# Two VectorE instruction forms in the routed octets of a relational graph convolution

## The chip, the cores and the metric

The kernel runs on one core of one Trainium2 chip. The metric is the device time of one execution, in microseconds, as the median of several runs. The core has five engines that run side by side: TensorE (PE; its weight loads are PEld), VectorE (DVE), ScalarE (ACT), GpSimd (POOL) and SyncE (SP). Each runs its own instructions in order; semaphores order work between engines. SBUF and PSUM are the two on-chip memories.

## The reference

The input is a graph with 12,500 nodes of 128 features and 200,000 edges in the order of their destination, each of one of 8 relations. Two layers of a relational graph convolution run one after the other, then a residual and a layer norm:

```python
def _rgcn_conv(x, src, dst, et, basis, comp, root, bias):
    W = einsum('rb,bio->rio', comp, basis)          # 8 matrices 128x128
    msgs = einsum('ni,rio->nro', x, W)[src, et]     # a row for each edge
    seg = dst * 8 + et
    mean = segment_sum(msgs, seg) / maximum(count(seg), 1)
    return mean.reshape(N, 8, 128).sum(1) + x @ root + bias
h = x
for l in range(2):
    h = relu(_rgcn_conv(h, src, dst, et, basis[l], comp[l], root[l], bias[l])) + h
return layernorm(x + h)
```

So each edge brings the row of its source node to a segment (destination, relation), weighted by one over the segment's count.

## The kernel before

The edges are cut into tiles of 128, one edge per partition, and eight tiles make an octet (`Q` is 8; there are 196 octets). A plan (`Plan`) records every operation with the cells that it reads and writes, puts in the semaphore waits, and then emits each engine's instructions in the recorded order.

In the first layer POOL gathers the source rows of a tile from the input with one indirect DMA (L752, `rows<-in_x_dram,idx`); its index column lies in SBUF. Behind each such gather `pause` (L709) waits for its previous pause and then writes zeros over 256 bytes per partition of an unused tile (L712, `blank<-`), which no engine reads. PE multiplies the rows by scaled one-hots that DVE makes (L1218), then by the relations' matrices (L1343), and places them at their nodes. As blocks of nodes become ready, a table `y_d` is written to HBM: for the second layer, the rows of every node times each of the eight matrices.

In the second layer two kinds of octets alternate. Most gather their eight tiles' rows from `y_d` (L752, `rows<-y_d,idy`), and DVE makes their one-hots by `slot_hots` (L1177, L1180) from a row of column numbers, `cols`, that lies in PSUM. Every third octet from 7 to 190, 62 in all, is routed (`ROUTED`, L510): its rows are not gathered but picked on the chip from `hT`, the first layer's result, which stays in SBUF, and POOL gathers only one tile of leftovers for it (`gather_left`, L774 to L782).

A routed octet's edges have been sorted, during the first layer, into 32 groups of three or four node blocks with 32 places each. It is worked off in four steps (`NU`), by `route_step` (L1930):

- `compare` (L1824) builds the one-hots that pick the rows. `bits`, an SBUF tile, holds for each of the step's 256 places (8 groups of 32) the edge's node within its block, as f16, the same in all partitions; `nodes` holds in column j each partition's own node number in the group's j-th block, as f32. For j = 0, 1, 2 one instruction compares the 256 places with column j and writes 256 f32 numbers to `hot_b` (home: the tile `dm`). In the last step of an octet, two groups have a fourth block: one more instruction over 64 places.
- `pick_rows` (L1865) multiplies these one-hots by `hT` on PE (L1880).
- `slots_in` (L1841) makes, for each of the step's two tiles of 128 picked rows, a one-hot of 640 columns: `segs`, the column numbers as f16 in SBUF (home: `y_row`), compared with the row's segment and scaled by the row's weight. Segment and weight are columns `v` and `NTL + v` of a small f32 SBUF tile (home: `comp_sb` or `sel`).
- `add_up` (L1891) multiplies the picked rows by these one-hots on PE (L1900) into two PSUM banks, and after the fourth step `relate` (L1918) applies the matrices.

At step t, `route_step` emits the comparison of step t+1, the picking of step t, the one-hots of step t−1 and the sums of step t−2. There are 248 steps. The line `steps_of.setdefault(FROM + t * EVERY // NU, [])` (L1951, `EVERY` 3, `NU` 4) spreads four steps over three octets, so that two of the four come together in one octet. POOL's gathers run up to five octets ahead (`AHEAD`, seven buffers `rows`).

Of the kernel before, what the change touches and what calls it, by code (L numbers as in the profile page):

```python
# [13 lines left out]
ALU = mybir.AluOpType  # L14
# [415 lines left out]
def ordered_path(  # L430
# [25 lines left out]
    nc = tc.nc  # L456
    P = 128
# [36 lines left out]
    CAP = 32  # L494
# [5 lines left out]
    NTL = NGR // BU  # L500
# [3 lines left out]
    SEG = R * NW  # L504
# [85 lines left out]
    def part_of(n, *cell):  # L590
        nonlocal free_at
        free_at += n
        assert free_at <= at
        sort_c.append(cell)
        return arena[:, free_at - n:free_at], cell
# [21 lines left out]
    left_b, idl_b, wl_b, nodes_b = (part_of(n, c) for n, c in ((4 * NR, "left"), (NR, "idl"), (NR, "wl"), (4, "nodes")))  # L617
# [57 lines left out]
    def vec(emit, reads=(), writes=()):  # L675
        plan.add("DVE", emit, reads, writes)
# [20 lines left out]
    def in_turn(emits):  # L697
        def emit():
            for e in emits:
                last = e()  # L700
            return last

        return emit
# [774 lines left out]
    nodes = nodes_b[0][:, :4]  # L1478
# [262 lines left out]
    segs = segs_b[0].bitcast(F16)  # L1741
# [6 lines left out]
    def new(cell):  # L1748

        if cell in touched:  # L1750
            return [cell]
        touched.add(cell)
        return [cell] + old[cell]
# [66 lines left out]
    def tiles_at(u):  # L1820

        return range(u * TU, (u + 1) * TU)

    def compare(t):  # L1824

        i, u = t // NU, t % NU
        if i >= NR:
            return
        n = GU * CAP
        (o, oc), (b, bc) = hot_b[t % 3], bits_b[i % 2]  # L1830
        bits = b.bitcast(F16)
        parts = [(j * n, u * n, n, j) for j in range(3)]
        more = [g for g in range(u * GU, (u + 1) * GU) if SIZE[g] > 3]
        if more:
            parts.append((3 * n, more[0] * CAP, len(more) * CAP, 3))
        vec(in_turn([lambda a=a, c=c, m=m, j=j: nc.vector.tensor_scalar(  # L1836
            o[:, a:a + m], bits[:, c:c + m], nodes[:, j:j + 1], None, op0=ALU.is_equal) for a, c, m, j in parts]),
            [bc, nodes_b[1]], new(oc))
        plan.mark("DVE")

    def slots_in(t):  # L1841

        i, u = t // NU, t % NU
        sg, sgc = segw_b[i % 2]
        for v in tiles_at(u):
            o, oc = slot_b[(i * NTL + v) % len(slot_b)]
            vec(lambda v=v, o=o: nc.vector.tensor_scalar(
                o, segs, sg[:, v:v + 1], sg[:, NTL + v:NTL + v + 1], op0=ALU.is_equal, op1=ALU.mult),
                [segs_b[1], sgc], new(oc))
        plan.mark("DVE")  # L1850

# [78 lines left out]
    def route_step(t):  # L1930

        i, u = t // NU, t % NU
        if u == 0 and i < NR:
            unit_rows(i)
        compare(t + 1)
        if i < NR:
            pick_rows(t)
        if 0 <= t - 1 < NR * NU:
            slots_in(t - 1)
        if 0 <= t - 2 < NR * NU:  # L1940
            add_up(t - 2)
        if u == 3 and i >= 1 and i - 1 < NR:
            relate(i - 1)
        if u == 1:
            fetch_rows(i + 1)
        if u == NU - 1:
            fetch(i + 2)
# [219 lines left out]
    def sup(q):  # L2167
        return (q * Q + G) // (2 * G) - 1
# [48 lines left out]
    def prep():  # L2217
        for i in range(1, len(groups)):
            if i + 1 < len(groups):
                sources(*groups[i + 1])  # L2220
                yield
            yield from counts(i)

    parts = prep()
# [46 lines left out]
    for o in range(NG - 3):  # L2271
# [7 lines left out]
        for i in range(2 if o < FIRST else 1):  # L2279
            if parts is not None and run(parts, 1):  # L2280
                parts = None
# [28 lines left out]
        if o > 1:  # L2310
            k = place(o - 2)
            close(k)
            if k is not None and k % S == S // 2 and k // S + 1 < NX:
                n = k // S + 1
                turned_to.extend([turn_x(n, h) for h in range(-(-shape_of(n)[1] // 4))])
                turned_to.append((lambda n=n: load_x(n + 1), None))
        for i in range(2):
            if turned_to:
                here = pt_b
                a, b = turned_to.pop(0)  # L2320
            elif tables and o >= TABLE and (i == 0 or len(tables) > 6 or o > NG - 16):
# [3 lines left out]
                a, b = tables.pop(0)(here)  # L2325
# [87 lines left out]
    for q in range(NQ):  # L2413
# [30 lines left out]
        if q == FROM - 1:  # L2444
            compare(0)
# [15 lines left out]
        for i in range(2):  # L2461
            for j, step in ending:
                step()
                plan.mark("DVE")
                n = j // S
# [10 lines left out]
            elif i == 0:  # L2476
                for j in [late] * (0 <= late < FULL) + [q] * (q >= FULL):
                    if opened_by(j)[1]:
                        a, b = finish(1, sup(j))
# [71 lines left out]
```

## Time and profile before

| | |
|---|---|
| median of 3 runs | 4073.62 us (4069.84 to 4075.93) |
| the profiled execution's own time | 4076.68 us |
| its span | 4074.9 us |
| busy share: PE, PEld, DVE, ACT, POOL | 74%, 60%, 54%, 16%, 88% |
| mean granted TensorE clock | 0.852 |
| POOL gathers, first and second layer | 1563 and 1067, 960 and 1005 ns each |
| leftovers' gathers (L777) | 62, 951 ns each |
| POOL memsets (L712) | 2692, 358 ns each |

A row of instructions in the profile names line, engine, operation, what is written from what is read, the shape, and the count; behind the bar stand busy microseconds and the mean nanoseconds of one, and behind the next the idle time before them with what ended it. "Issue" is idle time in which the engine waited for nothing that the profile shows. A row of the timeline gives an instruction's start and length in microseconds, then the same names; rows of the same kind in a row are merged (x3). Instructions of one engine can overlap a little in it. The second layer's gathers start at about 2297 us and end at about 4062 us.

### The profile page before, as it was taken

What the parts mean: (1) busy time and instruction counts of PE and PEld (TensorE: products, weight loads), DVE (VectorE), ACT (ScalarE), POOL (GpSimd) and SP (SyncE); (2) the same over time, 40 slices, a digit from 0 to 9 for tenths busy, and PEclk for the clock granted to TensorE, in tenths of its full rate; (3) what the DMA queues carried; (4) which work ended last, traced back from release to release, by engine and by line L of the source; (5) the groups of instructions that cost most, each with busy time, mean ns of one, the idle gap of its engine ahead of it and who ended that gap; (6) DMA issues with size and microseconds to landing.
All of it is one profiled execution on the core that took longest, in us unless ns stands there. A gap on an engine that the chain in (4) does not pass through costs nothing.

```text
span 4074.9 us, 70810 instructions
## 1 busy us (share of the span) xinstructions
PE 3029.9 (74%) x27639; PEld 2434.0 (60%) x27639; DVE 2191.0 (54%) x6800; ACT 666.3 (16%) x1725; POOL 3589.1 (88%) x5393
## 2 busy tenths in 40 slices
PE   6666666766666766676666659988888888888885
PEld 4555555655556666665555447666666666666663
DVE  6634343443267677774232247666656656556663
ACT  1111112112112222221221201111111111111110
POOL 8888888888888888888888788888888888888887
PEclk8988877777778778777887879998899999989997
DMA  3111122222222222222222322222222222222221
GB/s 117 51 46 46 46 66 87 87 85 77 82 67 67 68 63 66 72 67 69 87 77 82 124 53 55 66 64 55 61 65 54 64 64 58 59 64 64 54 59 54
DMA packets 134938, 276.02 MB, mean 68 GB/s; under 512 B 56995, under 2 KB 65741, under 8 KB 134597
## 3 DMA queue, kind: packets, MB, share of 16 engines
q0 software_dynamic: 86176, 176.66, 16.8%
q1 hardware_dynamic: 31450, 42.72, 3.5%
q10 hardware_dynamic: 16971, 52.05, 3.3%
q8 instruction: 219, 3.59, 0.4%
q14 instruction: 122, 1.00, 0.1%
HBM read 211.95 MB, written 59.28 MB: 67 GB/s over the span
## 4 chain that ended last, share of the span: by engine, by line
POOL 82%; issue 10%; PE 4%; DVE 1%; DMA 1%; ACT 1%; POOLq 0%; ACTq 0%; DVEq 0%
POOL rows L752 59%; POOL blank L712 22%; POOL arena L777 1%; PE s L1311 1%; DVE dm L1218 1%; PE pt L1442 0%; DVE arena L947 0%; PE y L1343 0%; PE pt L1880 0%; PE ct L957 0%; PE ct L958 0%; PE y L1900 0%; PE pt L905 0%; DMA arena<-in_dst_dram 0%; DMA rows<-y_d,idy 0%
## 5 line engine op out<-in xcount | busy, mean ns | idle before, releaser
L752 POOL DMA_INDIRECT rows<-in_x_dram,idx x1563 | 1500.0, 960 | 267.7 <-issue 264.6
L752 POOL DMA_INDIRECT rows<-y_d,idy x1067 | 1072.1, 1005 | 191.3 <-issue 176.3
L1311 PE MATMUL s<-dm,rows 128*128 128x128 f32 x3126 | 624.0, 381 | 611.7 <-DMA rows<-in_x_dram,idx 609.1
L1311 PEld LDWEIGHTS s<-dm,rows 128*128 128x128 f32 x3126 | 580.8, 286 | 681.6 <-issue 551.4
L712 POOL MEMSET blank<- 128x256 uint8 x2692 | 962.8, 358 | 1.5
L1218 DVE TENSOR_SCALAR dm<-cols,kr,w 128x128 f32<-128x128 f16 x1563 | 526.1, 403 | 314.8 <-PE ct L1442 180.3
L1343 PE MATMUL y<-w_sb,sT 128*128 128x128 f32 x3136 | 492.2, 323 | 46.4 <-ACT sT L692 46.4
L1343 PEld LDWEIGHTS y<-w_sb,sT 128*128 128x128 f32 x3136 | 481.3, 242 | 57.1 <-ACT sT L692 55.9
L1880 PE MATMUL pt<-arena,dm 128*32 128x128 f32 x12152 | 430.0, 293 | 44.2 <-DVE dm L1836 43.7
L1880 PEld LDWEIGHTS pt<-arena,dm 128*32 128x32 f32 x12152 | 354.3, 117 | 99.1 <-issue 82.8
L692 ACT ACTIVATE sT<-s 128x512 f32<-128x512 f32 x391 | 212.2, 594 | 1133.9 <-PE s L1311 1133.9
L1836 DVE TENSOR_SCALAR dm<-arena 128x256 f32<-128x256 f16 x806 | 267.2, 386 | 63.4 <-DMA arena<-y_d,arena 56.7
L1177 DVE TENSOR_SCALAR sT<-cols,kr,w 128x32 f32<-128x32 f16 x1040 | 238.3, 299 | 63.4 <-PE s L2021 63.2
L1900 PE MATMUL y<-arena,dm 128*128 128x320 f32 x620 | 246.8, 481 | 0.0
L1395 DVE TENSOR_TENSOR po<-po,carry 128x128 f32<-128x128 f32 x98 | 28.9, 295 | 396.9 <-PE ct L1442 193.5
L1986 PE MATMUL ct<-rows,sT 128*32 128x128 f32 x2080 | 99.2, 309 | 190.6 <-DMA rows<-y_d,idy 190.3
L1900 PE MATMUL po<-arena,dm 128*128 128x320 f32 x620 | 220.6, 438 | 0.0
L692 ACT ACTIVATE dm<-pt 128x256 f32<-128x256 f32 x248 | 95.4, 385 | 653.8 <-PE pt L1880 649.9
L1986 PEld LDWEIGHTS ct<-rows,sT 128*32 128x32 f32 x2080 | 59.7, 119 | 233.8 <-issue 120.2
L1395 DVE TENSOR_TENSOR s<-s,carry 128x128 f32<-128x128 f32 x97 | 28.5, 294 | 317.9 <-PE s L2017 214.5
L1900 PEld LDWEIGHTS po<-arena,dm 128*128 128x128 f32 x620 | 121.2, 195 | 52.5 <-issue 5.6
L692 ACT ACTIVATE y_row<-pt 128x512 f32<-128x512 f32 (+1 forms) x133 | 79.4, 597 | 433.7 <-PE ct L1442 194.6
(333 smaller groups left out, 3958.8 us busy)
## 6 DMA issues: line engine op xcount, KB each, us to landing
y_d<-y_row ACTq DMA_DIRECT2D x96, 512.0 KB
rows<-in_x_dram,idx POOLq DMA_INDIRECT x1563
rows<-y_d,idy POOLq DMA_INDIRECT x1067
arena<-lo_d SPq DMA_DIRECT2D x62, 256.0 KB
x_g<-in_x_dram SPq DMA_DIRECT2D x24, 512.0 KB
out_dram<-x_g SPq DMA_DIRECT2D x12, 512.0 KB
arena<-in_L_gnn_basis_dram SPq DMA_DIRECT2D x2, 512.0 KB
w_d<-y_row SPq DMA_DIRECT2D x2, 512.0 KB
```

The source lines that it names most:

```text
L692: act(lambda: nc.scalar.activation(out_t, in_t, AF.Copy), reads, writes)
L712: nc.gpsimd.memset(blank[:, :256], 0).then_inc(paused, 1)
L752: ins.append(nc.gpsimd.indirect_dma_start(out=t[:, i - q * Q, :], out_offset=None, in_=table_t, in_offset=bass.IndirectOffsetOnAxis(ap=ids ...
L1177: vec(in_turn([lambda i=i: nc.vector.tensor_scalar(t[:, i, :], cols[:, :2 * K], kr[:, i0 + i:i0 + i + 1], w[:, i0 + i:i0 + i + 1], op0=ALU ...
L1218: emits.append(lambda i=i: nc.vector.tensor_scalar(t[:, i - q * Q, :wide], cols[:, :wide], ids[:, i:i + 1], w[:, i:i + 1], op0=ALU.is_equa ...
L1311: last = nc.tensor.matmul(s_b[i // 4][0][:, i % 4, :], t[:, i, :], d[:, i, :], start=True, stop=True)
L1343: last = nc.tensor.matmul(y[:m], t[:, r, :nt, :].rearrange("p t k -> p (t k)"), w_sb[:, 0, r, :], start=(r == 0), stop=(r == R - 1))
L1395: emits.append(lambda: nc.vector.tensor_add(a[:, :n], a[:, :n], t[:, :n]))
L1836: vec(in_turn([lambda a=a, c=c, m=m, j=j: nc.vector.tensor_scalar(o[:, a:a + m], bits[:, c:c + m], nodes[:, j:j + 1], None, op0=ALU.is_equ ...
L1880: last = nc.tensor.matmul(b[k * CAP:(k + 1) * CAP, x, :], o[:n, c:c + CAP], hT[:n, j * P:(j + 1) * P], start=jj == 0, stop=jj == SIZE[g] - 1)
L1900: last = nc.tensor.matmul(b.rearrange("p t d -> p (t d)")[:, :SEG], g[:, x * P:(x + 1) * P], o[:, k * SEG:(k + 1) * SEG], start=v == 0, st ...
L1986: last = nc.tensor.matmul(m0[i // 2 * 2 * K:(i // 2 + 1) * 2 * K, :], d[:, i, :], t[:, i, :], start=i % 2 == 0, stop=i % 2 == 1)
```

## The change

In `compare`, the three instructions over 256 places become one `tensor_tensor` over 3 x 256: its first input is `bits`, repeated three times over the middle dimension, its second the first three columns of `nodes`, each spread over 256 places. The instruction for a fourth block becomes a `tensor_tensor` with the fourth column spread. In `slots_in`, the `tensor_scalar` with two per-partition scalars becomes a `scalar_tensor_tensor`: the segment stays a per-partition scalar, and the weight is the second tensor, one column spread over the 640. Inputs, outputs, types, tiles and the plan's reads and writes stay the same.

```diff
@@ compare
-        parts = [(j * n, u * n, n, j) for j in range(3)]
         more = [g for g in range(u * GU, (u + 1) * GU) if SIZE[g] > 3]
+        emits = [lambda: nc.vector.tensor_tensor(
+            o[:, :3 * n].rearrange("p (j c) -> p j c", j=3),
+            bits[:, None, u * n:(u + 1) * n].to_broadcast([P, 3, n]),
+            nodes[:, :3].unsqueeze(2).to_broadcast([P, 3, n]), op=ALU.is_equal)]
         if more:
-            parts.append((3 * n, more[0] * CAP, len(more) * CAP, 3))
-        vec(in_turn([lambda a=a, c=c, m=m, j=j: nc.vector.tensor_scalar(
-            o[:, a:a + m], bits[:, c:c + m], nodes[:, j:j + 1], None, op0=ALU.is_equal) for a, c, m, j in parts]),
-            [bc, nodes_b[1]], new(oc))
+            c, m = more[0] * CAP, len(more) * CAP
+            emits.append(lambda: nc.vector.tensor_tensor(
+                o[:, 3 * n:3 * n + m], bits[:, c:c + m], nodes[:, 3:4].to_broadcast([P, m]), op=ALU.is_equal))
+        vec(in_turn(emits), [bc, nodes_b[1]], new(oc))
@@ slots_in
-            vec(lambda v=v, o=o: nc.vector.tensor_scalar(
-                o, segs, sg[:, v:v + 1], sg[:, NTL + v:NTL + v + 1], op0=ALU.is_equal, op1=ALU.mult),
+            vec(lambda v=v, o=o: nc.vector.scalar_tensor_tensor(
+                o, segs, sg[:, v:v + 1], sg[:, NTL + v:NTL + v + 1].to_broadcast([P, 2 * SEG]), op0=ALU.is_equal,
+                op1=ALU.mult),
                 [segs_b[1], sgc], new(oc))
```

## The prediction

> **What bounds the kernel now.** I read the chain that ended last first, then POOL's groups in both halves of the run, then the timeline around single gathers. The chain, and the busy time of the engines in the second layer's stretch (its columns: stretch, its length, PE, PEld, DVE, ACT and POOL busy with counts, granted clock, DMA share, GB/s):
>
> ```profile
> POOL 82%; issue 10%; PE 4%; DVE 1%; DMA 1%; ACT 1%; POOLq 0%; ACTq 0%; DVEq 0%
> 2310.00:4060.00 1750.00, 1458.85 (x18250) 1082.97 (x18248) 1057.68 (x3441) 226.48 (x682) 1563.23 (x2238) 0.91 0.23 61
> ```
>
> POOL carries the chain. In the second layer it is busy for 1563 of 1750 us, and what is left is the 0.16 us between an instruction and the next that its rows call "issue". It waits for nobody there, so what POOL loses per gather is lost to the end, and what another engine gains is not seen. POOL's own groups, first layer (0 to 2290 us), then second (2310 to 4060 us):
>
> ```profile
> L752 POOL DMA_INDIRECT rows<-in_x_dram,idx x1563 | 1500.0, 960 | 267.7 <-issue 264.6 <-DMA arena<-in_dst_dram 2.1 <-PE y L1343 0.5
> L712 POOL MEMSET blank<- 128x256 uint8 x1563 | 514.9, 329 | 1.0
> ...
> L752 POOL DMA_INDIRECT rows<-y_d,idy x1057 | 1062.6, 1005 | 174.8 <-issue 174.8
> L712 POOL MEMSET blank<- 128x256 uint8 x1118 | 444.4, 397 | 0.5
> L777 POOL DMA_INDIRECT arena<-y_d,arena x62 | 59.0, 951 | 10.2 <-issue 9.7 <-PE po L1922 0.5
> ```
>
> An undisturbed cycle is 0.95 (gather) + 0.33 (memset) + 0.16 (issue) = 1.44 us. The second layer is above it by 1062.6 − 1057×0.951 = 57 us in gathers and 444.4 − 1118×0.329 = 77 us in memsets: 134 us. The timeline shows beside what:
>
> ```profile
> 2414.59 1.29 DVE L1836 TENSOR_SCALAR dm<-arena 128x256 f32<-128x256 f16 x3
> 2415.64 2.11 POOL L752 DMA_INDIRECT rows<-y_d,idy  x1 [0.16 <-issue]
> 2415.80 0.60 DVE L1847 TENSOR_SCALAR arena<-y_row,sel 128x640 f32<-128x640 f16 x1
> 2416.32 0.60 DVE L1847 TENSOR_SCALAR sT<-y_row,sel 128x640 f32<-128x640 f16 x1
> ...
> 2399.37 1.22 DVE L1847 TENSOR_SCALAR arena<-y_row,sel 128x640 f32<-128x640 f16 x2
> 2400.27 0.57 POOL L712 MEMSET blank<- 128x256 uint8 x1
> ```
>
> Gather and memset both stretch beside the two lines that change. I take off 3 us, an estimate, for the few other DVE operations beside which POOL stretches: the old forms cost 131 us.
>
> **The change, part by part.**
>
> *DVE's own time.* What goes, and the nearest rows for what comes:
>
> ```profile
> L1836 DVE TENSOR_SCALAR dm<-arena 128x256 f32<-128x256 f16 x744 | 255.5, 396 | 63.4 <-DMA arena<-y_d,arena 56.7 <-DMA arena<-lo_d 5.9 <-ACT dm L692 0.9
> 2310.00:4060.00 1750.00, 306.41 (x496) 0.91 0.23 61
> 2310.00:4060.00 1750.00, 267.16 (x806) 0.91 0.23 61
> L1630 DVE TENSOR_TENSOR arena<-arena 128x768 f16<-128x768 f16 x62 | 59.6, 961 | 2.1
> L1525 DVE SCALAR_TENSOR_TENSOR arena<-arena 128x496 f32<-128x496 f16 x1 | 0.7, 678 | 0.0
> L1395 DVE TENSOR_TENSOR s<-s,carry 128x128 f32<-128x128 f32 x97 | 28.5, 294 | 317.9 <-PE s L2017 214.5
> L1399 DVE TENSOR_SCALAR carry<-s,bias_t 128x128 f32<-128x128 f32 x97 | 33.1, 341 | 0.0
> ```
>
> (The second and third row are all of L1847 and L1836, overlaps taken out: 306 + 267 = 573 us.) The new comparison does 768 elements in one instruction. L1630 is the same shape, one operand repeated over the middle dimension and the other spread: 0.96 us, so 768 elements at 1.04 ns and 0.16 fixed. The 62 extra comparisons of 64 elements become 0.07 + 0.16 = 0.23 us. The scaled one-hot, 640 elements, at L1525's rate (496 in 0.678) is 0.667 + 0.161; a per-partition scalar adds 0.341 − 0.294 = 0.047; together 0.875 us (bounds: 0.60, as L1847 runs undisturbed above, and 1.0). Back-to-back instructions overlap by 0.08 us (2416.32 starts 0.08 before 2415.80 + 0.60). A step is then 0.88 + 2×0.795 = 2.47 us, times 248 steps, with the extra comparisons 621 us: 48 more than now. DVE goes from 1058 to 1106 of 1750 us (63%). That is hidden by the 37% left and by the order: a step's slots serve the sums one step later. Were that cover gone, it would cost up to 48 us. No instruction is added on POOL, SP or PE; no wait is added or moved.
>
> *The memsets.* Rows of the first layer show memsets and gathers beside a tensor_tensor with both inputs in SBUF; the gather comes after its start, before it, and 0.04 us after it:
>
> ```profile
> 1157.75 0.33 POOL L712 MEMSET blank<- 128x256 uint8 x1
> 1157.93 0.96 DVE L1630 TENSOR_TENSOR arena<-arena 128x768 f16<-128x768 f16 x1
> 1158.24 1.47 POOL L752 DMA_INDIRECT rows<-in_x_dram,idx  x1 [0.16 <-issue]
> ...
> 1168.87 0.95 POOL L752 DMA_INDIRECT rows<-in_x_dram,idx  x1 [0.17 <-issue]
> 1169.15 0.96 DVE L1630 TENSOR_TENSOR arena<-arena 128x768 f16<-128x768 f16 x1
> 1169.82 0.33 POOL L712 MEMSET blank<- 128x256 uint8 x1
> ...
> 575.91 0.36 DVE L1045 TENSOR_TENSOR arena<-arena 128x128 f32<-128x128 f32 x1
> 575.95 0.95 POOL L752 DMA_INDIRECT rows<-in_x_dram,idx  x1 [0.17 <-issue]
> ```
>
> The memsets keep 0.33: their 77 us go. A gather that starts during such an operation ends 0.82 us after it (1158.89, then 1159.71), so it stands still from 0.13 us after its start to the operation's end; one that started earlier keeps 0.95.
>
> In the Trainium skill, "SBUF — State Buffer", section "Who interferes with whom", a DVE instruction with two SBUF inputs contends with a GpSimd instruction that reads SBUF, and not with one that only writes it; the trace agrees (0.33 beside it, 1.47 beside it). This rule speaks against the change: both new forms have two SBUF inputs.
>
> *The gathers.* An operation that starts 0.04 us ahead of the gather does not hold it (575.95), so a hold runs from some 0.13 + 0.04 = 0.17 us after the operation's start to its end. So a comparison holds for 0.79 us, a one-hot for 0.70. With independent phases an operation costs hold²/(2×1.44): 0.217 and 0.170 us, a step 0.557, all 248 steps 138 us (128 if the scalar's 0.047 us holds nothing). But the three operations follow each other. Counting from a step's start they hold from 0.17 to 0.96, 1.05 to 1.75 and 1.84 to 2.55. A request at 0.3 waits 0.66, and the next, 1.44 after the release, waits 0.15; one at 1.0 waits nothing, and the next 0.11. Over all phases a single step comes to 0.46 us; two steps in a row (62 of the 186 places, since EVERY is 3 and NU 4) to 0.75. Sum: 124×0.46 + 62×0.75 = 104 us.
>
> That supposes that a held gather gets in at the first operation's end. It may not:
>
> ```profile
> 667.59 0.28 DVE L1040 TENSOR_TENSOR arena<-arena 128x128 f32<-128x128 int32 x1
> 667.73 1.17 POOL L752 DMA_INDIRECT rows<-in_x_dram,idx  x1 [0.17 <-issue]
> 667.79 0.29 DVE L1042 TENSOR_TENSOR arena<-arena 128x128 f32<-128x128 int32 x1
> ...
> 679.33 0.28 DVE L1040 TENSOR_TENSOR arena<-arena 128x128 f32<-128x128 int32 x1
> 679.47 0.96 POOL L752 DMA_INDIRECT rows<-in_x_dram,idx  x1 [0.17 <-issue]
> 679.52 0.29 DVE L1042 TENSOR_TENSOR arena<-arena 128x128 f32<-128x128 int32 x1
> ...
> 543.64 1.33 POOL L752 DMA_INDIRECT rows<-in_x_dram,idx  x1 [0.16 <-issue]
> 543.67 0.28 DVE L1040 TENSOR_TENSOR arena<-arena 128x128 f32<-128x128 int32 x1
> 543.87 0.29 DVE L1042 TENSOR_TENSOR arena<-arena 128x128 f32<-128x128 int32 x1
> ```
>
> The same pair lets a gather in at the first end once (0.96) and at the second twice (1.17, 1.33); 2415.64 above was held to the end of the second L1847 (2416.92, and 0.82 later it ends). I take two in three lost where a comparison follows (62 places × 0.45 asking × 0.67 × 0.88 = 16 us), and, as 2415.64 is rare in the timeline, 3% elsewhere (some 370 held × 0.03 × 0.8 = 9 us). At 543.64 the operation started 0.03 us after the gather and held it all the same: one that follows another without a break seems to hold 0.1 us sooner, 186 × 0.1/1.44 × 0.84 = 11 us. New cost: 104 + 16 + 9 + 11 = 140 us, estimates all.
>
> **Sum.** Gone 131, new 140: +9 us. The profiled execution took 4076.7 us (span 4074.9), 3.1 above the median of the runs, 4073.6. So 4085.7 for it and **4082.6 us** for the median. What a measurement can tell from no change here is about 0.2%, 8 us.
>
> **The rivals.**
> 1. *Faster: a held gather always gets in at the first end.* Then 100 to 118 us (104 to the cycle-stretched 128×1.44/1.56) replace 131: −13 to −31, say 4052 us. For it: 679.47 and most gathers beside L1836 (mean 1005 against 951, far from whole trains). It decides from where the losses above stay under 27 us.
> 2. *Slower by much: a gather is often held to the end of the train of operations,* as at 2415.64 and 667.73. Held always, a single step costs about 1.7 us in the mean and a double one 4.2: 470 us at most, 4410; at one loss in five, some 165 to 170 us, 4110. Against: the 0.96 at 679.47. A one-hot slower than one element per 1.04 ns works the same way: at 1.0 us it holds 0.83, and the independent sum rises to 173 us.
> 3. *Faster by much: the spread operand doesn't hold the gather.* For the one-hots alone only 248×0.217 = 54 us are new: −77, 3997; for both, −131, 3943. Against it stands 1158.24. The same section of the skill infers that descriptor generation needs the write interface only; by that the time would be 3943, and 1158.24 disagrees.
>
> **How the numbers follow.** Forecast 0.44 (own range 4066 to 4105, of it 0.13 within 0.2%), rival 1 0.28 (0.02 within 0.2%), rival 2 0.22, rival 3 0.06. So faster 0.32, same 0.15, slower 0.53. The range 4040 to 4140 leaves out rival 3 and about half of rival 2.
>
> **What would show it.** Second-layer memsets at a mean of 0.33 us (now 0.397): step one. Gathers at 0.951 + 140/1057 = 1.08 (now 1.005): step two; under 1.06 rival 1, over 1.11 rival 2, 1.00 or less rival 3. The comparison at 0.96, the one-hot at 0.87. No POOL wait but "issue". The prediction is wrong if the one-hots run far from 0.87 or if PE or POOL begins to wait for DVE.

## The result and the profile after

The changed kernel takes 4108.15 us (median of 4 runs, 4105.95 to 4110.31) against 4074.47 us for the kernel before on the same chip: a ratio of 1.0085, 95% interval 1.0067 to 1.0102. It is slower by 34 us where 9 were forecast. Its profiled execution took 4105.95 us (span 4104.2), 29.3 above that of the kernel before.

The chain that ended last; the busy times in the second layer's stretch (columns as in the prediction); the same for all one-hots (L1850) and all extra comparisons (L1839) alone; POOL's groups there; and the comparison's group:

```profile
POOL 83%; issue 10%; PE 5%; DMA 1%; ACT 0%; DVE 0%; POOLq 0%; ACTq 0%
2310.00:4085.00 1775.00, 1462.28 (x18227) 1086.23 (x18225) 1138.45 (x2944) 225.35 (x681) 1588.45 (x2229) 0.90 0.22 60
2310.00:4085.00 1775.00, 415.04 (x496) 0.90 0.22 60
2310.00:4085.00 1775.00, 13.29 (x62) 0.90 0.22 60
...
L752 POOL DMA_INDIRECT rows<-y_d,idy x1052 | 1165.3, 1108 | 174.5 <-issue 174.5
L712 POOL MEMSET blank<- 128x256 uint8 x1114 | 366.3, 329 | 0.7
L777 POOL DMA_INDIRECT arena<-y_d,arena x62 | 59.1, 954 | 10.2 <-issue 9.9 <-PE po L1926 0.2 <-PE po L1904 0.2
...
L1833 DVE TENSOR_TENSOR dm<-arena 128x768 f32<-128x768 f16 x248 | 232.4, 937 | 63.4 <-DMA arena<-y_d,arena 56.2 <-DMA arena<-lo_d 5.7 <-ACT dm L692 1.5
L1850 DVE SCALAR_TENSOR_TENSOR arena<-y_row,comp_sb 128x640 f32<-128x640 f16 x155 | 130.9, 875 | 0.2
L1850 DVE SCALAR_TENSOR_TENSOR idx<-y_row,comp_sb 128x640 f32<-128x640 f16 x62 | 52.1, 879 | 0.0
```

POOL still carries the chain and still waits for nothing but "issue". The memset is back at 329 ns from 397, and the gather went from 1005 to 1108 ns. Over the whole second layer (1130 gathers, 1129 memsets), time above an undisturbed instruction went from 81.0 to 4.3 us in the memsets and from 58.7 to 166.3 us in the gathers: −77 and +108, net +31, beside the 29.3 us between the two profiled executions. DVE is busy for 1138 of 1775 us, and POOL never waits for it.

Where the gathers' 166 us lie can be read from each held gather: it ends 0.82 us after the DVE operation that held it, so the release is known, and so is the first DVE end after its request. The time up to that first end is what the prediction called the hold; whatever is beyond it is a lost handover. Summed over the 348 held gathers (where the sorting draws its limits moves single rows by one or two gathers and up to 2 us):

| part | gathers | us | predicted |
|---|---|---|---|
| held up to the first end: one-hots | 222 | 59.2 | |
| held up to the first end: comparisons | 126 | 49.8 | 104 + 11 in all |
| lost: comparison, then both one-hots | 24 | 38.3 | |
| lost: one-hot, then a comparison | 7 | 6.1 | |
| lost: comparison, then the extra comparison | 28 | 3.8 | |
| lost: one-hot, then the other one-hot | 4 | 3.2 | 16 + 9 in all |
| not matched to one of these operations | | 5.6 | |

One stretch of the timeline shows three of the kinds (the row of 1.68 us is a step's two one-hots, the second from 2479.71 to 2480.59):

```profile
2477.91 0.95 DVE L1833 TENSOR_TENSOR dm<-arena 128x768 f32<-128x768 f16 x1
2478.15 1.67 POOL L752 DMA_INDIRECT rows<-y_d,idy  x1 [0.17 <-issue]
2478.78 0.22 DVE L1839 TENSOR_TENSOR dm<-arena 128x64 f32<-128x64 f16 x1
2478.91 1.68 DVE L1850 SCALAR_TENSOR_TENSOR arena<-y_row,comp_sb 128x640 f32<-128x640 f16 x2
...
2480.31 1.10 POOL L752 DMA_INDIRECT rows<-y_d,idy  x1 [0.17 <-issue]
...
2481.55 0.95 DVE L1833 TENSOR_TENSOR dm<-arena 128x768 f32<-128x768 f16 x1
...
2481.90 3.01 POOL L752 DMA_INDIRECT rows<-y_d,idy  x1 [0.17 <-issue]
...
2482.41 0.88 DVE L1850 SCALAR_TENSOR_TENSOR arena<-y_row,comp_sb 128x640 f32<-128x640 f16 x1
...
2483.21 0.88 DVE L1850 SCALAR_TENSOR_TENSOR sT<-y_row,comp_sb 128x640 f32<-128x640 f16 x1
```

The gather at 2478.15 ends at 2479.82, so it was let in at 2479.00: not when the comparison ended (2478.86) but when the extra comparison did. The one-hot that had started at 2478.91 did not hold it any longer. The next gather asks 1.44 us after that release, at 2480.44, and waits 0.15 us for the one-hot that ends at 2480.59: this is the second wait of 0.15 that the prediction worked out. The gather at 2481.90 was let in at 2484.09, at the end of the second one-hot. It stood still through a comparison and two one-hots, 2.06 us instead of the 0.47 to the end of the comparison. There are 24 such gathers.

### The profile page after: what moved, and what is told of

It is laid out like the page before. It is cut to its first block, busy times and chain, and to the rows that moved or that the text cites. A ratio compares the mean times of both kernels' runs of the same rounds, so it can differ in the third digit from the quotient of the medians.

```text
span 4104.2 us, 70314 instructions
## 1 busy us (share of the span) xinstructions
PE 3034.8 (74%) x27639; PEld 2438.4 (59%) x27639; DVE 2272.4 (55%) x6304; ACT 665.6 (16%) x1725; POOL 3618.2 (88%) x5393
## 4 chain that ended last, share of the span: by engine, by line
POOL 83%; issue 10%; PE 5%; DMA 1%; ACT 0%; DVE 0%; POOLq 0%; ACTq 0%
POOL rows L752 61%; POOL blank L712 20%; POOL arena L777 1%; PE pt L1884 1%; PE y L1904 1%; PE y L1343 1%; PE pt L1442 1%; PE po L1904 1%; PE s L1311 1%; PE po L1926 0%; DMA rows<-in_x_dram,idx 0%; ACT y_row L692 0%; PE s L2021 0%; DMA rows<-y_d,idy 0%; PE pt L1114 0%
## 5 line engine op out<-in xcount | busy, mean ns | idle before, releaser
L752 POOL DMA_INDIRECT rows<-y_d,idy x1067 | 1179.5, 1105 | 190.9 <-issue 176.8
L712 POOL MEMSET blank<- 128x256 uint8 x2692 | 885.4, 329 | 1.7
L1833 DVE TENSOR_TENSOR dm<-arena 128x768 f32<-128x768 f16 x248 | 232.4, 937 | 63.4 <-DMA arena<-y_d,arena 56.2
```

Source lines behind the costliest of these rows:

```text
L712: nc.gpsimd.memset(blank[:, :256], 0).then_inc(paused, 1)
L752: ins.append(nc.gpsimd.indirect_dma_start(out=t[:, i - q * Q, :], out_offset=None, in_=table_t, in_offset=bass.IndirectOffsetOnAxis(ap=ids ...
L1833: emits = [lambda: nc.vector.tensor_tensor(o[:, :3 * n].rearrange("p (j c) -> p j c", j=3), bits[:, None, u * n:(u + 1) * n].to_broadcast( ...
```

## The experiments

Two theories were set against each other. By the first, what sets the time is how long a gather stands still beside a VectorE operation that reads two operands from SBUF. By the second, it is VectorE's own time, which the change lengthens, however well it seems hidden. Within the first theory the question was where the loss beyond the forecast lies.

In the session of the first four runs, and in that of the last one, the kernel before itself took 4577 and 4252 us, and in the traces of those runs POOL waits for PE in the second layer; those times are not used as prices, and the four were run again in another session.

| kernel | us | before | ratio (95%) | gathers' excess, us | memsets' excess, us |
|---|---|---|---|---|---|
| before (its profile) | 4076.7 | | | 58.7 | 81.0 |
| after | 4108.15 | 4074.47 | 1.0085 (1.0067 to 1.0102) | 166.3 | 4.3 |
| comparisons alone | 4059.66 | 4074.14 | 0.9964 (0.9951 to 0.9976) | 78.8 | 47.6 |
| one-hots alone | 4073.19 | 4074.14 | 0.9999 (0.9989 to 1.0008) | 116.0 | 18.5 |
| after, nodes in PSUM | 4048.70 | 4074.14 | 0.9939 (0.9923 to 0.9956) | 105.5 | 4.0 |
| after, column numbers in PSUM | 4014.19 | 4074.14 | 0.9852 (0.9835 to 0.9868) | 74.5 | 4.0 |
| after, both in PSUM | 3946.32 | 4072.21 | 0.9687 (0.9671 to 0.9704) | 3.1 | 3.9 |
| the same, one-hots as before | 3944.95 | 4072.21 | 0.9687 (0.9671 to 0.9704) | 3.2 | 3.9 |
| after, gaps everywhere | 4104.57 | 4072.21 | 1.0077 (1.0060 to 1.0094) | 167.0 | 5.7 |

"Excess" is the time above 0.950 us for each of the 1130 gathers and above 0.325 us for each of the 1129 memsets of the second layer.

### The comparisons alone, the one-hots alone

Each is the kernel before with one half of the diff: `compare` as after and `slots_in` as before (`cmp_only`), or the other way round (`slots_only`).

> The comparisons in the new form, the scaled one-hots in the old one. Hold theory (a gather stands still from its start to the end of a DVE operation with two SBUF inputs; the old forms hold gathers and memsets): the new comparisons hold gathers for about 50 to 55 us in all, as they do in the changed kernel, and take away the old comparisons' part of 131 us, by their share of DVE's time some 60 us. So 4060 to 4085 us; second-layer memsets still above 0.33 us in the mean, since L1847 is still there. DVE-time theory (the change is slower because DVE works longer): DVE loses some 20 us of work, so no slower than before, 4074 or a little less.

> The scaled one-hots in the new form, the comparisons in the old one. Hold theory: the new one-hots hold gathers for about 60 us and take away some 70 us; the trains held from a new comparison over both one-hots (38 us in the changed kernel) cannot come in this form, so 4065 to 4095 us, and the two halves together fall short of the 34 us that the whole change costs. DVE-time theory: DVE works some 109 us longer than before, more than in the changed kernel, so 4108 us or more.

In the first session they took 4624.53 (ratio 1.0101) and 4563.63 us (0.9975) against 4577.0. Neither is a price of the change, as the profiles show. The chain that ended last with the comparisons alone, and the gather of L777 there:

```profile
PE 54%; another core or an unknown queue 21%; issue 12%; DVE 6%; ACT 4%; POOL 2%; DMA 0%; ACTq 0%; POOLq 0%; DVEq 0%
...
L777 POOL DMA_INDIRECT arena<-y_d,arena x62 | 59.0, 952 | 523.6 <-PE po L1797 278.6
```

POOL has 2% of this chain and stands idle for 524 us ahead of that gather, where it stood idle for 10 before. What it loses or gains per gather cannot be seen in the end time. The chain's 21% are waits whose releaser the profile could not name; what slowed PE in that session is not shown. So the same two kernels ran again:

> The comparisons in the new form, the one-hots in the old one, again, since the kernel before took 4577 us beside the first run of this and POOL waited for PE there. Hold theory: the new comparisons hold gathers for some 50 to 55 us, the old one-hots keep some 70 us of their own; against 131 before, 4060 to 4085 us. DVE-time theory: DVE works some 20 us less than before, so 4074 us or a little less.

> The one-hots in the new form, the comparisons in the old one, again for the same reason. Hold theory: the new one-hots hold gathers for some 60 us or more, the old comparisons keep some 60; no train is held over a comparison and two one-hots, so 4065 to 4100 us, and this run's loss and the one of cmp_only_2 together fall short of the 34 us of the whole change. DVE-time theory: DVE works 109 us longer than before, more than in the changed kernel, so 4108 us or more.

POOL's groups in the second layer, comparisons alone:

```profile
L752 POOL DMA_INDIRECT rows<-y_d,idy x1058 | 1082.7, 1023 | 175.5 <-issue 175.5
L712 POOL MEMSET blank<- 128x256 uint8 x1120 | 411.6, 368 | 0.6
```

and one-hots alone:

```profile
L752 POOL DMA_INDIRECT rows<-y_d,idy x1057 | 1119.6, 1059 | 174.3 <-issue 174.3
L712 POOL MEMSET blank<- 128x256 uint8 x1119 | 382.2, 342 | 0.6
```

The comparisons alone gain 14.5 us, just past the expected 4060, and the one-hots alone change nothing that can be measured (−1 us), inside the expected 4065 to 4100 and far from the 4108 that VectorE's time would give. Each moves POOL's loss from the memsets to the gathers, and the sum of both excesses falls by 13 and 5 us. Both halves together should then give −15.5; they give +34. So some 50 us of the change belong to neither half alone. The table divides them. The memsets' excess falls by 33 us in one half and by 62 in the other, 96 in all, though only 77 go with both: 19 of the 50 us are memset time that either half frees. The gathers' excess rises by 20 and 57 us in the halves and by 108 with both: the other 30. Sorted as above, gathers held from a comparison over both one-hots cost 7 us with the comparisons alone and 9 with the one-hots alone (5 gathers, though the expectation had ruled such trains out), and 38 with both; most of the 30 lies there.

### One operand moved to PSUM

If two SBUF operands are what holds a gather, one operand in PSUM should free it, with VectorE's time left as it is. `bank`, a PSUM tile, has words that only the first layer uses; a copy at the start of the routes fills them. For the one-hots (`segs_psum`), the column numbers:

```diff
+    segs_p = bank[:, P:P + SEG].bitcast(F16)
...
-                o, segs, sg[:, v:v + 1], sg[:, NTL + v:NTL + v + 1].to_broadcast([P, 2 * SEG]), ...
-                [segs_b[1], sgc], new(oc))
+                o, segs_p, sg[:, v:v + 1], sg[:, NTL + v:NTL + v + 1].to_broadcast([P, 2 * SEG]), ...
+                ["keyp", sgc], new(oc))
...
+        vec(lambda: nc.vector.tensor_copy(bank[:, P:P + SEG], segs_b[0].bitcast(I32)), [segs_b[1]], ["keyp"])
```

For the comparisons (`nodes_psum`), the four node numbers of each partition, which are the spread operand:

```diff
+    nodes_p = bank[:, 480:484].bitcast(F32)
...
-            nodes[:, :3].unsqueeze(2).to_broadcast([P, 3, n]), op=ALU.is_equal)]
+            nodes_p[:, :3].unsqueeze(2).to_broadcast([P, 3, n]), op=ALU.is_equal)]
...
+        vec(lambda: nc.vector.tensor_copy(nodes_p, nodes), [nodes_b[1]], ["nodes_p"])
```

> The changed kernel, with the comparisons' spread second input read from PSUM in place of SBUF: one SBUF input is left. Hold theory: the comparisons (0.94 us as before) hold nobody; their 50 us of first holds and the 42 us of trains that begin with them go, some of those gathers are then held by a one-hot instead. 4010 to 4040 us. DVE-time theory: DVE's time is the same, so 4108 us.

> The changed kernel, with the scaled one-hots' first input (the column numbers) read from PSUM in place of SBUF: one SBUF input is left. Hold theory: the one-hots (0.87 us, perhaps 0.06 more from PSUM) hold nobody; their 59 us and the trains' 47 us go, the comparisons' 50 us stay. 3995 to 4025 us. DVE-time theory: 4108 us or a little more.

These, too, first ran where POOL was not the bound: 4628.45 (1.0105) and 4733.32 us (1.0356) against 4577.0. The gathers' and memsets' excess in their traces was 60 and 32 us, where the two halves of the change had 69 and 88 in the same session, so gathers were freed there as well; why the second of them still lost 3.6% in that session is not known. Run again:

> The changed kernel with the comparisons' spread input from PSUM, again for the same reason. Hold theory: comparisons hold nobody; their 50 us of first holds and the 42 us of trains that begin with them go, some of these gathers are then held by a one-hot: 4010 to 4040 us. DVE-time theory: 4108 us.

> The changed kernel with the one-hots' column numbers from PSUM, again for the same reason. Hold theory: one-hots hold nobody; their 59 us and the 47 us lost over trains go, the comparisons' 50 us stay: 3995 to 4025 us. DVE-time theory: 4108 us or a little more.

The gathers' groups in the second layer, nodes in PSUM first and column numbers in PSUM second:

```profile
L752 POOL DMA_INDIRECT rows<-y_d,idy x1057 | 1109.1, 1049 | 175.7 <-issue 175.4 <-PE pt L1885 0.2 <-PE po L1927 0.2
```

```profile
L752 POOL DMA_INDIRECT rows<-y_d,idy x1057 | 1077.4, 1019 | 175.7 <-issue 175.5 <-PE pt L1885 0.2
```

Freeing the one-hots brings 4014.19, as expected (3995 to 4025), though the holds up to a comparison's first end rose to some 64 us where 50 were expected. Freeing the comparisons brings 4048.70, 9 us outside the expected 4010 to 4040. Its trace says why: the gathers that no longer wait for a comparison wait for the one-hot behind it. Holds up to a one-hot's first end rise from 59.2 to 82.4 us, and 20 gathers lose the handover between the two one-hots (16.0 us). A hold that is taken away is partly passed on to what follows in the same train.

With both operands in PSUM (`both_psum`):

> The changed kernel, with one input of each new form read from PSUM: the comparisons' spread operand and the one-hots' column numbers. Hold theory: neither holds a gather or a memset, second-layer gathers 0.95 to 0.96 us and memsets 0.33 in the mean; 4108 - 163 = 3945 us (3935 to 3960), far below the kernel before. DVE-time theory: DVE works as long as in the changed kernel, so 4108 us or more.

```profile
L752 POOL DMA_INDIRECT rows<-y_d,idy x1054 | 1004.2, 953 | 175.2 <-issue 174.9 <-PE po L1799 0.2 <-PE s L2025 0.2
L712 POOL MEMSET blank<- 128x256 uint8 x1116 | 366.5, 328 | 0.7
...
2310.00:3925.00 1615.00, 1406.89 (x18240) 1048.57 (x18240) 1132.89 (x2941) 226.29 (x682) 1427.82 (x2233) 0.94 0.25 66
...
L1835 DVE TENSOR_TENSOR dm<-arena,cols 128x768 f32<-128x768 f16 x248 | 231.7, 934 | 5.5 <-DMA arena<-lo_d 3.4 <-ACT dm L692 2.1
L1852 DVE SCALAR_TENSOR_TENSOR arena<-cols,comp_sb 128x640 f32<-128x640 f16 x155 | 131.0, 879 | 37.2 <-DMA arena<-y_d,arena 37.2
```

This settles the cause. (POOL's two groups, the stretch's busy times, and the two VectorE groups, all of the second layer.) VectorE does the same operations at the same durations, 934 and 879 ns, and is busy for 1133 us as after (1138). The gather is at 953 ns, and the kernel takes 3946.32 us. The theory of VectorE's own time is dead: that time did not change, and 162 us went. In the Trainium skill, "SBUF — State Buffer", section "Who interferes with whom", an instruction of VectorE with at most one SBUF input, outside its two-port modes, does not contend with GpSimd; the trace agrees (gathers at 953 ns beside it). This version is faster than both kernels, by 3.1% than the kernel before.

Last, the same with the one-hots as `tensor_scalar` again, from PSUM (`both_psum_ts`):

> As the run before, but the scaled one-hots are tensor_scalar again, as in the kernel before, with the column numbers from PSUM. One SBUF input and two per-partition scalars: by the rows of L1203 some 0.667 + 0.26 = 0.93 us each, so DVE works 25 us longer than with scalar_tensor_tensor. Hold theory: nothing is held, the same 3945 us (3935 to 3960). If it is the instruction's kind and not the place of its inputs that holds, memsets and gathers are held as before: 4074 us or more.

```profile
L752 POOL DMA_INDIRECT rows<-y_d,idy x1057 | 1007.1, 953 | 175.7 <-issue 175.5 <-PE pt L1885 0.2
L712 POOL MEMSET blank<- 128x256 uint8 x1119 | 367.6, 328 | 0.7
...
L1852 DVE TENSOR_SCALAR arena<-cols,comp_sb 128x640 f32<-128x640 f16 x155 | 140.5, 941 | 37.1 <-DMA arena<-y_d,arena 37.0
```

It takes 3944.95 us, as expected, though a one-hot now takes 941 ns where it took 879. With the column numbers in PSUM, both instruction forms leave POOL alone. With them in SBUF the forms are not alike: beside the old ones memsets stretch too (397 ns before, 329 after). The old form also ran faster from SBUF, as this row of the kernel before shows:

```profile
L1847 DVE TENSOR_SCALAR arena<-y_row,comp_sb 128x640 f32<-128x640 f16 x155 | 96.4, 652 | 0.2
```

Why the old form, with one tensor in SBUF beside its two per-partition scalars, holds gathers and memsets there was not tested. The one-hots' scalars alone do not do it: they lie in SBUF in this run too.

### Gaps between the operations

The lost handovers were the first suspect for the 50 us. In `gaps`, each comparison and each one-hot waits for the operation before it, so that 0.035 us lie between them in place of the overlap of 0.08:

```diff
-        vec(in_turn(emits), [bc, nodes_b[1]], new(oc))
+        vec(in_turn(emits), [bc, nodes_b[1], "turn"], new(oc) + ["turn"])
...
-                [segs_b[1], sgc], new(oc))
+                [segs_b[1], sgc, "turn"], new(oc) + ["turn"])
```

> The changed kernel, where each comparison and each one-hot also waits for the end of the one before it, so that they no longer overlap by 0.08 us but stand 0.03 apart. Handover theory (a held gather is lost only where the next operation overlaps the end): the 24 gathers held over comparison, one-hot and one-hot (38 us), and the others held over two (9 us) get in at the first end; 4108 - 47 = 4061 us (4045 to 4080), though DVE works up to 80 us longer. Against it: the gather loses for another reason, or DVE's longer time counts: 4108 us or more.

It took 4104.57 us: a clear miss. A stretch of its timeline:

```profile
2444.21 0.94 DVE L1833 TENSOR_TENSOR dm<-arena 128x768 f32<-128x768 f16 x1
2444.57 1.41 POOL L752 DMA_INDIRECT rows<-y_d,idy  x1 [0.17 <-issue]
2445.19 0.89 DVE L1850 SCALAR_TENSOR_TENSOR arena<-y_row,comp_sb 128x640 f32<-128x640 f16 x1
2445.98 0.33 POOL L712 MEMSET blank<- 128x256 uint8 x1
2446.11 0.89 DVE L1850 SCALAR_TENSOR_TENSOR sT<-y_row,comp_sb 128x640 f32<-128x640 f16 x1
2446.47 1.35 POOL L752 DMA_INDIRECT rows<-y_d,idy  x1 [0.17 <-issue]
```

The gather at 2444.57 is let in at 2445.16, when the comparison ends. So it is everywhere: not one handover from a comparison to a one-hot, between one-hots, or from a one-hot to a comparison is lost (204 won). Only those from a comparison to its extra comparison, which this edit leaves without a gap, are lost, 34 of them, 4.6 us. But the wait up to the first end went from 109.0 to 158.9 us, and the same timeline shows how. The next gather asks 1.44 us after the release, at 2446.60, and the second one-hot ends at 2447.00: it waits 0.40. Before the edit two ends lay 2×0.795 = 1.59 us apart, and the wait was 0.15; with the gaps they lie 2×0.92 = 1.84 apart. 195 gathers of this run are held for 0.4 to 0.5 us. Adding up the phases as the prediction did, with these distances, gives 149 us (and 105 for the kernel after, measured 109): the expectation of 4061 had left the old 0.15 in the sum.

So the last kernel puts the gap at one place only: the first one-hot of a step waits for the comparison (`gap_cs`).

```diff
-        vec(in_turn(emits), [bc, nodes_b[1]], new(oc))
+        vec(in_turn(emits), [bc, nodes_b[1]], new(oc) + ["turn"])
...
-                [segs_b[1], sgc], new(oc))
+                [segs_b[1], sgc] + ["turn"] * (v == u * TU), new(oc))
```

> The changed kernel, where only the first one-hot of a step waits for the end of the comparison before it; the two one-hots and the next comparison still overlap. Phase account: a held gather asks again 1.44 us after the end that let it in, so what it waits next is set by where the following ends lie. With a gap of 0.035 us in this one place the sum over all phases is 0.533 us for a single step and 0.922 for two in a row, 124 x 0.533 + 62 x 0.922 = 123 us (105 for the changed kernel, whose rows have 109; 149 for the run with gaps everywhere, whose rows have 159). The 24 gathers held over a whole train (38 us) get in at the comparison's end, the other lost handovers (13 us) stay. So 109 + 51 becomes some 127 + 13: 20 us less, 4088 us (4075 to 4095). If gaps do nothing, 4108; if they only cost, 4108 or more.

Its time, 4210.80 us against 4252.2 in that session (ratio 0.9914, 0.9885 to 0.9942), is no price, since POOL waited for PE there:

```profile
L752 POOL DMA_INDIRECT rows<-y_d,idy x1061 | 1128.4, 1064 | 208.0 <-issue 175.3 <-PE ct L1990 32.7
L777 POOL DMA_INDIRECT arena<-y_d,arena x62 | 61.2, 986 | 95.5 <-PE po L1797 74.9 <-PE s L2025 13.7 <-issue 4.1
```

Its trace answers the question about the hold all the same, for instance here:

```profile
2447.04 0.95 DVE L1833 TENSOR_TENSOR dm<-arena 128x768 f32<-128x768 f16 x1
2447.40 1.42 POOL L752 DMA_INDIRECT rows<-y_d,idy  x1 [0.17 <-issue]
...
2448.02 0.88 DVE L1850 SCALAR_TENSOR_TENSOR arena<-y_row,comp_sb 128x640 f32<-128x640 f16 x1
...
2448.82 0.88 DVE L1850 SCALAR_TENSOR_TENSOR sT<-y_row,comp_sb 128x640 f32<-128x640 f16 x1
```

This gather started 0.36 us after its comparison, nearly as the one at 2481.90 did (0.35), and was let in at 2448.00, when the comparison ended. All 66 handovers from a comparison to a one-hot were won, 11 to an extra comparison were lost (1.5 us), and the holds up to the first end were 115.3 us where 127 were expected. The waits for PE also move the gathers against the operations, so this is no test of that sum. The gathers' excess was 122.9 us where the kernel after has 166.3. What that is worth in time where POOL is the bound was not measured.

## Why the prediction was right and wrong

The sign and the mechanism were right; the size was off by 25 us. The measured 4108 lies inside the wide range (4040 to 4140), which takes in about half of rival 2, and 3 us above the forecast's own range (4066 to 4105). By its steps:

- *Durations.* Right. Comparison 0.937 us (0.96 predicted), extra comparison 0.215 (0.23), one-hot 0.877 (0.875). The rival of a one-hot of 1.0 us falls.
- *VectorE's time.* "48 us more" was measured as 81 (1057.68 to 1138.45). The same rows as the prediction's give 232.4 + 13.3 + 415.0 = 661 us against 573, so +87. The prediction had taken the 0.08 us of overlap between operations of different lines out of the new sum (621), some 40 us of it, but not out of the old one. It did no harm: with the same VectorE time the kernel with both operands in PSUM takes 3946 us.
- *The memsets.* Right: 77 us were to go, 76.7 went.
- *The hold up to the first end.* Right: 104 + 11 = 115 us predicted, 109.0 measured, in 348 gathers of the "some 370". That it came out so closely is partly luck: the sum spreads the gathers' starts evenly, and in the trace they are bunched: of 132 gathers that started beside a comparison, 30 started between 0.60 and 0.65 us after it began.
- *The lost handovers.* This is the step that failed: "3% elsewhere (some 370 held × 0.03 × 0.8 = 9 us)". With the 16 us for places where a comparison follows, 25 us were predicted, and 51.4 measured. The two terms were also put at the wrong places. One-hot to comparison cost 6.1 us and comparison to extra comparison 3.8; comparison to one-hot, which was "elsewhere", cost 38.3. Of some 90 gathers that asked during such a comparison, about one in four lost; where a comparison followed, 7 of 35 did, not two in three. And the price of a loss was not one operation's 0.8 us but the rest of the train, 38.3/24 = 1.6 us each.
- *Sum.* 109.0 + 51.4 + 5.6 = 166 us of new cost against 140 predicted: the missing 26 are the lost handovers. Less the 131 of the old forms this is +35; the excess over the whole second layer gave +31, and the medians show +34.
- *Rival 1* (always let in at the first end, 4052) falls: 63 losses. The gaps show that even with nearly no losses its number does not follow, because the edit that kept handovers from being lost also moved the operations against the gathers' cycle.
- *Rival 2* (held to the end of the train) was partly true, and in its milder form closer than the forecast. Its 4110 at one loss in five is within 2 us of the measured time, its new cost of 165 to 170 us holds the measured 166, and 63 of the 348 held gathers (18%) lost a handover. But the losses are not spread evenly over the places, and a mean gather of 1108 ns stayed just under the mark of 1.11 set for it.
- *Rival 3* (the spread operand doesn't hold the gather) falls: both new forms hold it. Its 3943 us is what one gets by taking the operand out of SBUF (3946).

What stays open: why a handover is lost from a comparison to a one-hot (one in four) and almost never between one-hots (4 in the kernel after, though 20 with the nodes in PSUM). Between operations with a gap no loss was seen; what decides the single case where they overlap isn't shown. Chance alone it is not. In the kernel after, 18 of the gathers that lost such a handover had started 0.35 us after their comparison, where only 2 won, and none of the 24 that had started 0.60 us after it lost. The overlap differs too, 69 to 78 ns in nearly all losses and 80 to 88 in nearly all wins, but from a one-hot to a comparison it is the other way round (losses at 83 to 87 ns, wins at 73 to 84), so neither is shown to be the cause. Of the 50 us that neither half has alone, the gathers' 30 are not a loss that can be taken out by itself: the kernel with gaps has nearly no lost handovers and is as slow. And what made POOL wait for PE in two sessions is not known.

## What to carry to other kernels

Where gathers on GpSimd are the bound, look first at where the VectorE instructions beside them read: with one operand of each new form in PSUM, 162 us went, and from then on neither the form nor a one-hot longer by 62 ns cost anything. Where an operation still holds gathers, its duration counts, and the form can: in SBUF the old and the new ones held different things. Price a train of such operations as a whole: the halves were worth −14.5 and −1 us, and both together +34. A blocked engine comes back one cycle after its release, so what it costs depends on how that cycle (1.44 us) stands to the distance of the operations' ends, and an edit that moves these ends by 0.1 us can give back all that it saves.

## What the runs showed of the hardware beyond what was expected

- A gather that loses the handover from a comparison to a one-hot loses the next one as well: all 24 stood to the end of the second one-hot (3.01 us, as at 2481.90, for most), though a gather that first asks during a one-hot nearly always gets in at its end. It is not so after other losses: the 28 held on by an extra comparison, and the 7 held on by a comparison, got in at its end, although a one-hot followed with the same overlap each time.
- A gap of 0.035 us is enough: with it none of 204 handovers was lost, and none of the 66 from a comparison to a one-hot in the last run, against about one in four of these with an overlap of 0.08.
- The place of one operand costs the new forms nothing: a comparison took 937 ns with its spread operand in SBUF and 934 with it in PSUM, a one-hot 877 and 879. For the old form it does: 652 ns for a one-hot from SBUF in the kernel before, 941 with the column numbers in PSUM.
